# A graph layer and a mixture of experts: the first two node tiles go through all eight experts unsorted

## The chip, the cores and the metric

The kernel runs on one core of one Trainium2 chip. A core has TensorE (PE: matmuls and transposes), VectorE (DVE), ScalarE (ACT), GpSimd (POOL) and SyncE (SP, which here only issues transfers). Each has its own queue of instructions and takes them in order; they wait for one another through semaphores. Transfers run on 16 DMA engines. The metric is the device time of one execution in microseconds (us).

## The reference

There are 6250 nodes of 256 features, 100000 edges of which only the first 6250 matter to the output, and eight experts. Cut to what matters:

```python
def gnn(x, edge_index, weight, attn_l, attn_r):       # 4 heads of 64
    xt = (x @ weight).reshape(-1, 4, 64)
    alpha_l = einsum('ehd,hd->eh', xt[row], attn_l)
    alpha_r = einsum('ehd,hd->eh', xt[col], attn_r)
    alpha = softmax(leaky_relu(alpha_l + alpha_r, 0.01), axis=1)
    tmp = einsum('nh,nhd->nd', alpha[:n], xt[col[:n]])
    return broadcast_to(tmp[:, None, :], (n, 4, 64)).reshape(n, 256)

def moe(tokens, router_w, w1, b1, w2, b2):
    probs = softmax(tokens @ router_w.T)
    rw, re = top_k(probs, 2);  rw = rw / rw.sum(-1)
    combine = zeros((n, 8)).at[arange(n)[:, None], re].set(rw)
    out = tokens
    for e in range(8):
        h = gelu(tokens @ w1[e] + b1[e])               # 256 -> 256
        out = out + combine[:, e:e+1] * (h @ w2[e] + b2[e])
    return out

x = x + gnn(layernorm(x), stack([src, dst]), ...)
return x + moe(layernorm(x), ...)
```

Each node needs two of the eight experts. All of it is in float32.

## The kernel before

The nodes lie in 49 tiles of 128. The work is a straight program, written out in the order in which every engine is to take it; no scheduler reorders it. It has four stages.

**Setup and source terms** (to about 48 us). The rows of x, the edges and the graph weight are loaded, and per node the source side of the attention and the router's share of the node's own row are computed.

**Features** (48 to 139 us). The 49 tiles come in five groups, `GROUPS`, of 10, 10, 9, 10 and 10. GpSimd gathers the rows of the destination nodes; TensorE turns them (`turn`), multiplies them by the graph weight (`features`) and looks up the source terms (`look_up`); ScalarE copies each product and squares each row; VectorE does the attention and the routing. The work after the matmuls of a group is spread over the tiles of the next one by `tasks(g)`: `attend_1`, `exponents` (ScalarE), `attend_2`, `attend_3` and the five steps of `route` for group g-1, `rank` (TensorE) and `ranked` (VectorE) for group g-2. `put(i, what)` sets the tile after which a piece stands. `route` finds the two best experts of each node, writes the group's finished rows into `table` in DRAM, and marks in `mine_all` which of the 28 pairs of experts the node belongs to. `rank` counts, with matmuls of ones, how many nodes of the same pair come earlier. `feature_root` is a power on GpSimd at the end of each group, which `attend_1` needs.

**The sort** (139 to 191 us). The last group has no next one to hide in: `attend_1(z)`, `exponents(z)`, `rank(z - 1)`, `ranked(z - 1)`, `attend_2(z)`, `attend_3`, `route(z)`, `rank(z)`, `ranked(z)` come one after the other. Then VectorE turns the ranks into places (`place`), and with one-hot tables in bfloat16 (`of_lane`, `of_slice`, `by`, in three passes) and 49 matmuls (`pi`) the places are inverted: `held_by` names the node in each place. The nodes now lie in 49 slices of 128, ordered by pair. The pairs follow the path `PATH`, in which neighbours share an expert, so that a slice holds few experts. A slice and an expert that it needs make a *unit*; there are at most 2 x 49 + 28 - 1 = 125, `NU`. `pf` (16 matmuls) makes the list of units; VectorE turns it into integers, `for_act`, `for_pe` and `for_dve`, that the engines read as registers. A Gelu on one element (`warm`) brings ScalarE's table in early, and `keep_on(26)` issues 26 matmuls whose results nobody reads.

**The sorted units** (191 to 433 us). `fetch` gathers sorted rows from `table` (an indirect DMA on GpSimd), `norm` normalizes them on VectorE, GpSimd and ScalarE, and `turn_slice` turns them. For unit u, `fill` loads the expert's first matrix (256 KB, on SP's queue, 4 units ahead, six buffers), `first` does its 4 matmuls and two Gelus, and `second`, two units later, the 2 matmuls by `we2` (all experts' second matrices, held in `big`) and two scaled additions into `acc` on VectorE. `finish` scatters a slice's rows to the output with an indirect DMA. The queue of SP between the stages holds, in this order: the table write of group 3 (L593), the one of group 4, the register load of `for_act` (L1051), and the loads of the first units (L1079).

Memory is reused across stages: `early.close()` frees the tiles of the first three stages, and the tiles of the units (`late`) lie where those were.

Of the kernel before, what the change touches and what calls it, by code (L numbers as in the profile page):

```python
# [9 lines left out]
FP = mybir.dt.float32  # L10
BF = mybir.dt.bfloat16
# [11 lines left out]
def kernel(  # L23
# [35 lines left out]

    nc = tc.nc  # L60
    N, D = x.shape
# [21 lines left out]
    NS = -(-N // TS)  # L83
# [17 lines left out]
    assert sum(n for _, n in GROUPS) == NT == NS and HD == D and F == D and NE == 8  # L101
    assert 96 <= LAST < P

    const = ctx.enter_context(tc.tile_pool(name="const", bufs=1))
# [14 lines left out]


# [10 lines left out]
    held_by = const.tile([TS, NS], I32, name="held_by")  # L131

# [20 lines left out]
    mine_all = held.tile([P, NT, NPAIR], BF, name="mine_all")  # L153
    rank_all = held.tile([P, NT], FP, name="rank_all")
    outside = held.tile([P, 1], FP, name="outside")

    NTE = NT + NT % 2
    high_1 = held.tile([P, NTE * P], BF, name="high_1")
# [396 lines left out]
    table = dram.tile([NT * P, R], FP, name="table")  # L555
# [3 lines left out]
    def route(g):  # L559
# [33 lines left out]
        nc.sync.dma_start(table_v[:, at, :], row)  # L593
# [3 lines left out]
        mine = mine_all[:, at, :]  # L597
        nc.vector.tensor_tensor(mine, long(pairs, n), wide(pair, NPAIR), ALU.is_equal)
# [6 lines left out]
    def rank(g):  # L605


        n, mine = GROUPS[g][1], mine_all[:, group(g), :]
# [14 lines left out]
    def ranked(g):  # L623
        n, pk = GROUPS[g][1], ranks.pop(g)
# [4 lines left out]
        nc.vector.tensor_tensor(mr, pk[:, :n, :], mine_all[:, group(g), :], ALU.mult)  # L629
        nc.vector.tensor_reduce(rank_all[:, group(g)], mr, AX.X, ALU.add)  # L630
        if g == NG - 1:
            nc.vector.tensor_tensor(
                rank_all[:, NT - 1 :], rank_all[:, NT - 1 :], outside, ALU.add
            )
# [73 lines left out]
    count_b = mid.tile([P, NTE], BF, name="count_b", bufs=1)  # L708
    def counting():
# [5 lines left out]
            count_b, pattern=[[1, NTE]], base=0, channel_multiplier=0,  # L715
            allow_small_or_imprecise_dtypes=True,
        )

# [7 lines left out]
    def tasks(g):  # L726
# [22 lines left out]
        if g == 3:  # L749
            put(0, load_experts)  # L750
        if g == 4:
            put(0, load_biases)
        return at
# [30 lines left out]
    n = GROUPS[z][1]  # L784
    attend_1(z)
    exponents(z)
    rank(z - 1)
    ranked(z - 1)
# [14 lines left out]

    warm = small.tile([P, 1], FP, name="warm", bufs=1)
    nc.scalar.activation(warm, exs[z][:, 0, :1], AF.Gelu)
# [9 lines left out]
    ms = work.tile([P, NT, NPAIR], FP, name="ms", tag="pxs")  # L815
    for g in range(NG):
        nc.vector.tensor_tensor(
            ms[:, group(g), :], mine_all[:, group(g), :],
# [7 lines left out]
    for k, (op, by) in enumerate(  # L826
# [5 lines left out]
        if NTE > NT:  # L832
            nc.vector.memset(part[:, NT:], -1.0)
# [366 lines left out]
```

## Time and profile before

| | |
|---|---|
| median of 9 runs | 441.67 us (439.25 to 442.88) |
| the profiled execution | 444.69 us, its span 442.9 us |
| mean granted TensorE clock | 0.931 |
| TensorE matmul, busy | 377.1 us (85%) |
| VectorE, busy | 311.0 us (70%) |
| ScalarE, busy | 224.9 us (51%) |
| GpSimd, busy | 200.6 us (45%) |
| last look-up matmul ends / first sorted unit starts | 138.92 / 190.97 us |

Line numbers L... are those of the kernel before. In a group of the profile, `out<-in` names what an instruction writes and reads; PE is a matmul, PEld a weight load. One float32 matmul is counted as two, so a unit's `first` is 8 and its `second` 4. The granted clock is 1.00 where TensorE runs at full speed and 0.50 at half. The chain of waits is the work that ended last, followed back from the end: an engine that is not in it had time to spare there.

### The profile page before, as it was taken

To read this page: it belongs to the slowest core of one execution; us is meant where nothing else is said; L and a number is where in the kernel's file an instruction comes from. 1 tells how busy PE (TensorE), PEld (TensorE's weight loads), DVE (VectorE), ACT (ScalarE), POOL (GpSimd) and SP (SyncE) were. 2 spreads that over 40 slices of the span, in tenths; PEclk is the share of its full clock that TensorE was granted. 3 is DMA by queue.
4 is the path that set the end of the run, shared out by engine and by line. 5 is a ranking of instruction groups with operands and counts; after the bars stand their busy time and mean duration, and the time that the engine had idled before them with its cause. 6 is when DMAs were issued, how large, how long until landed. Compare 5 with 4: busy or idle time off the path is not lost.

```text
span 442.9 us, 9881 instructions
## 1 busy us (share of the span) xinstructions
PE 377.1 (85%) x2576; PEld 323.6 (73%) x2576; DVE 311.0 (70%) x1083; ACT 224.9 (51%) x658; POOL 200.6 (45%) x240
## 2 busy tenths in 40 slices
PE   6977869998995018878999999999998999999991
PEld 4754648776784016467999998888887899999990
DVE  5979512889879987537888778778677877655551
ACT  3454547865773100056666666656556567433330
POOL 0075867888222000543434366657556643332222
PEclk9996999999999555689999999999999999999997
DMA  7978443473971440386666676667766656666620
GB/s 228 354 202 109 78 84 63 88 214 109 295 222 53 144 156 0 97 243 165 195 182 180 196 228 184 219 206 218 218 191 206 202 186 191 180 183 193 187 71 22
DMA packets 59108, 74.63 MB, mean 169 GB/s; under 512 B 7170, under 2 KB 54102, under 8 KB 58800
## 3 DMA queue, kind: packets, MB, share of 16 engines
q1 hardware_dynamic: 51504, 52.45, 38.9%
q0 software_dynamic: 7248, 21.29, 18.9%
q8 instruction: 23, 0.38, 0.3%
q10 hardware_dynamic: 304, 0.27, 0.2%
q14 instruction: 29, 0.24, 0.2%
HBM read 59.13 MB, written 14.87 MB: 167 GB/s over the span
## 4 chain that ended last, share of the span: by engine, by line
PE 69%; DVE 16%; issue 5%; ACT 3%; DMA 2%; POOL 1%; another core or an unknown queue 1%; SPq 1%; POOLq 0%; ACTq 0%
PE ph L1091 26%; PE py L1107 23%; PE px L468 6%; PE pt L246 4%; DVE pxs L544 3%; PE pt L1037 2%; DVE pxs L549 2%; PE pa L422 2%; PE pl L497 1%; DVE x L550 1%; PE pi L856 1%; ACT tT L250 1%; DMA w<-in_L_ffn_w_dram 1%; DVE ag L505 1%
## 5 line engine op out<-in xcount | busy, mean ns | idle before, releaser
L1091 PEld LDWEIGHTS ph<-tokT,w 128*128 128x128 f32 x1000 | 131.1, 194 | 18.9 <-issue 5.4
L1091 PE MATMUL ph<-tokT,w 128*128 (+1 forms) x1000 | 134.6, 278 | 7.4 <-ACT tokT L1038 2.1
L1107 PE MATMUL py<-big,hid 128*128 x500 | 128.9, 381 | 0.0
L1098 ACT ACTIVATE hid<-ph,b_cols 128x128 f32<-128x128 f32 x250 | 78.5, 366 | 84.3 <-PE ph L1091 67.0
L1107 PEld LDWEIGHTS py<-big,hid 128*128 128x128 f32 x500 | 85.4, 191 | 7.4 <-DVE acc L1114 0.6
L914 POOL DMA_INDIRECT xr<-table,held_by x49 | 49.8, 1017 | 74.3 <-DVE held_by L901 39.2
L1114 DVE SCALAR_TENSOR_TENSOR acc<-py,shares,acc 128x256 f32 (+1 forms) x125 | 60.5, 484 | 32.3 <-PE py L1107 13.7
L1118 POOL DMA_INDIRECT out_dram<-acc,held_by x49 | 51.0, 1040 | 54.8 <-DVE acc L1114 39.7
L1114 DVE SCALAR_TENSOR_TENSOR acc<-big,shares,acc (+1 forms) x125 | 60.2, 481 | 11.0 <-issue 5.3
L468 PE MATMUL px<-w_sb,tT 128*128 128x293 f32 x196 | 57.2, 423 | 4.1 <-issue 3.8
L1004 ACT ACTIVATE tok<-xr,nm 128x256 f32<-128x256 f32 x49 | 29.4, 602 | 58.1 <-DVE nm L1000 41.1
L468 PEld LDWEIGHTS px<-w_sb,tT 128*128 128x128 f32 x196 | 34.7, 193 | 12.2 <-issue 4.7
L235 POOL DMA_INDIRECT big<-in_x_dram,dst_sb x31 | 33.0, 1064 | 7.9 <-issue 7.2
L250 ACT COPY tT<-pt 128x512 f32<-128x512 f32 (+2 forms) x56 | 27.3, 528 | 14.6 <-PE pt L246 13.2
L476 ACT COPY pxs<-px 128x293 f32<-128x293 f32 x49 | 19.7, 403 | 27.9 <-PE px L468 17.1
L978 DVE TENSOR_TENSOR xr<-xr 128x512 f32<-128x512 f32 (+1 forms) x25 | 17.2, 689 | 17.6 <-issue 17.5
L1014 ACT ACTIVATE acc<-xr,nm 128x256 f32<-128x256 f32 x49 | 29.1, 597 | 0.0
L505 DVE TENSOR_REDUCE ag<-pl 128x8 f32<-128x392 f32 (+1 forms) x25 | 13.8, 552 | 18.2 <-PE pl L501 12.7
L993 POOL TENSOR_SCALAR mv<-mv 128x2 f32<-128x2 f32 (+1 forms) x25 | 5.6, 225 | 39.0 <-DVE mv L990 35.2
L235 POOL DMA_INDIRECT xd_own<-in_x_dram,dst_sb x18 | 19.3, 1070 | 4.9 <-issue 4.1
L246 PE MATMUL pt<-ident,x 128*128 128x128 f32 x98 | 17.3, 328 | 4.5 <-ACT tT L250 2.3
L497 PE MATMUL pl<-al_sb,high 128*128 128x196 bf16 x147 | 19.2, 251 | 1.9 <-DVE ag L505 1.9
(210 smaller groups left out, 479.8 us busy)
## 6 DMA issues: line engine op xcount, KB each, us to landing
w<-in_L_ffn_w_dram SPq DMA_DIRECT2D x125, 256.0 KB
table<-x SPq DMA_DIRECT2D x4, 1685.0 KB
x<-in_x_dram SPq DMA_DIRECT2D x10, 512.0 KB
big<-in_L_ffn_w_dram SPq DMA_DIRECT2D x2, 1024.0 KB
high<-highs SPq DMA_DIRECT2D x1, 1568.0 KB
table<-x SPq DMA_DIRECT2D x1, 1516.5 KB
big<-in_L_ffn_b_dram SPq DMA_DIRECT2D x1, 1024.0 KB
xr<-table,held_by POOLq DMA_INDIRECT x49
```

The source lines that it names most:

```text
L235: nc.gpsimd.indirect_dma_start(out=xd(t), out_offset=None, in_=x[:, :], in_offset=bass.IndirectOffsetOnAxis(ap=dst_sb[:, t : t + 1], axis=0),)
L246: nc.tensor.transpose(pt[:, i * P : (i + 1) * P], of(t0 + i)[:, c * 128 : (c + 1) * 128], ident)
L250: nc.scalar.copy(tT, pt)
L468: nc.tensor.matmul(px, blocks[c][:, k * P : (k + 1) * P], w_sb[:, c, :], start=(c == 0), stop=(c == DC - 1),)
L914: nc.gpsimd.indirect_dma_start(out=xr[:, i, :], out_offset=None, in_=table[:, :], in_offset=bass.IndirectOffsetOnAxis(ap=held_by[:, s0 + i ...
L1004: nc.scalar.activation(tok[:, i, :], xr[:, i, :D], AF.Identity, bias=bias[:, i : i + 1], scale=scale[:, i : i + 1],)
L1014: nc.scalar.activation(acc[:, s * D : (s + 1) * D], xr[:, i, :D], AF.Identity, bias=bias[:, i : i + 1], scale=more[:, i : i + 1],)
L1091: nc.tensor.matmul(ph[:, j, :], w[:, c * F + j * 128 : c * F + (j + 1) * 128], tokT[:, bass.ds(rows_at + c * TS, TS)], start=(c == 0), sto ...
L1098: nc.scalar.activation(hid[:, j, :], ph[:, j, :], AF.Gelu, bias=b1_cols[:, :, j][:, bass.ds(at_act[u][0], 1)])
L1107: nc.tensor.matmul(py, hid[:, j, :], we2[:, j, bass.ds(at_pe[u][1], D)], start=(j == 0), stop=(j == FC - 1),)
L1114: nc.vector.scalar_tensor_tensor(to, y, share, to, op0=ALU.mult, op1=ALU.add)
L1118: nc.gpsimd.indirect_dma_start(out=ends_at[s][:, :], out_offset=bass.IndirectOffsetOnAxis(ap=held_by[:n, s : s + 1], axis=0), in_=acc[:n, ...
```

## The change

Tiles 0 and 1 of the nodes no longer take part in the sort. Their rows stay in SBUF (`xs[0]`), and after the features they go through all eight experts, with a share of 0 for the six that a node does not use: 16 unsorted units, `UNSORTED`. For the rest there are 47 tiles and slices (`NTS`, `NS`), so `NU` is 121, and every table of the sort is narrower by two columns. `group(g)` becomes `sorted_of(g)` where sorted tiles are meant.

- `load_unsorted` loads the eight first matrices (2 MB) and b2 on SP's queue into memory of groups 1 and 2 that is free by then: six matrices in group 3, two and b2 in group 4.
- `complete`, `sums`, `squares`, `scaled` do the layer norm of the two tiles on GpSimd and ScalarE, among the tiles of group 4.
- `turn_unsorted` turns them; `unsorted_shares` makes the shares; `unsorted_units(n)` takes n steps of the 17: step k is `unsorted_first(k)`, then `unsorted_second(k - 1)`. A result is copied out of PSUM with its share as scale by ScalarE (`y`, three buffers) and added to `d_acc` by GpSimd.
- The steps are put between the pieces of the sort, 2 + 2 + 3 + 4 + 1 + 5, with the bias terms after the fourth. The last five take the place of 20 of the 26 matmuls of `keep_on`.
- `warm` moves ahead, to just behind `exponents(z)`.
- At the end of the last step the two tiles are stored, on SP's queue.
- `finish` scatters by `held_out`, the places moved by 256 rows.

```diff
-    NS = -(-N // TS)
+    ND = 2
+    NTS = NT - ND
+    NS = -(-(N - ND * P) // TS)
     NU = 2 * NS + NPAIR - 1
...
+    UNSORTED = [(d, e) for d in range(ND) for e in range(NE)]
...
+    def load_unsorted(k):
+        e0, e1 = ((0, 6), (6, NE))[k]
+        of = held.tile([128, (12, 11)[k] * D], FP, name=f"unsorted{k}", tag=f"x{k + 1}")
+        for e in range(e0, e1):
+            w1_parts[e] = of[:, (e - e0) * DC * F : (e - e0 + 1) * DC * F]
+            nc.sync.dma_start(w1_parts[e].rearrange("p (c f) -> p c f", f=F),
+                w1[e : e + 1, :, :].rearrange("o (c p) f -> p (o c) f", p=128))
...
+            nc.sync.dma_start(d_of["b2"], b2)
+    def complete():
+        for d in range(ND):
+            v = d_row[:, d, :D].rearrange("p (h k) -> p h k", k=OC)
+            nc.gpsimd.tensor_tensor(
+                v, v, d_row[:, d : d + 1, U : U + OC].to_broadcast([P, H, OC]), ALU.add)
+    def sums():
+        for d in range(ND):
+            nc.scalar.activation(
+                d_y[0], d_row[:, d, :D], AF.Identity, accum_out=d_sum[:, d : d + 1])
+        nc.gpsimd.tensor_scalar(d_mean, d_sum, -ROOT_D / D, None, ALU.mult)
+    def squares():
...
+        root(d_scale, d_var)
...
+    def scaled():
+        for to, by in ((d_tok, d_scale), (d_acc, d_more)):
+            for d in range(ND):
+                nc.scalar.activation(to[d], d_row[:, d, :D], AF.Identity,
+                    bias=d_bias[:, d : d + 1], scale=by[:, d : d + 1])
+    def turn_unsorted():
...
+    def unsorted_shares():
+        nc.scalar.activation(d_second, d_log, AF.Tanh, scale=0.5)
...
+    def unsorted_first(k):
+        d, e = UNSORTED[k]
+        w, tokT = w1_parts[e], d_of["tokT"]
+        ph = ps.tile([128, FC, P], FP, name="ph4", tag="m")
...
+        hid = d_of["hid"][k % 3]
+        for j in range(FC):
+            nc.scalar.activation(hid[:, j * P : (j + 1) * P], ph[:, j, :], AF.Gelu,
+                bias=b1_cols[:, e, j : j + 1])
+    def add_to(d, k, py, scale):
+        y = d_y[k % 3]
+        nc.scalar.activation(y, py, AF.Identity, scale=scale)
+        nc.gpsimd.tensor_tensor(d_acc[d], d_acc[d], y, ALU.add)
+    def unsorted_second(k):
...
+        add_to(d, k, py, d_share[:, d, e : e + 1])
+    def unsorted_biases():
+        for d in range(ND):
+            pt = ps.tile([NE, P], FP, name="pt5", tag="t")
+            nc.tensor.transpose(pt, d_share[:, d, :], ident)
+            to = d_of["shareT"][:, d * P : (d + 1) * P]
+            nc.scalar.copy(to, pt)
+            py = ps.tile([P, D], FP, name="py5", tag="t")
+            nc.tensor.matmul(py, to, d_of["b2"], start=True, stop=True)
+            add_to(d, d, py, 1.0)
+    def unsorted_units(n):
+        for k in range(gone[0], min(gone[0] + n, len(UNSORTED) + 1)):
+            if k < len(UNSORTED):
+                unsorted_first(k)
+            if k > 0:
+                unsorted_second(k - 1)
+        gone[0] += n
+        if gone[0] == len(UNSORTED) + 1:
+            for d in range(ND):
+                nc.sync.dma_start(out_parts[NS][d * P : (d + 1) * P, :], d_acc[d])
...
         if g == 3:
             put(0, load_experts)
+            put(5, lambda: load_unsorted(0))
         if g == 4:
             put(0, load_biases)
+            put(1, lambda: load_unsorted(1))
+            for i, what in ((1, complete), (3, sums), (5, squares), (8, scaled)):
+                put(i, what)
...
+    turn_unsorted()
     attend_1(z)
     exponents(z)
+    warm = small.tile([P, 1], FP, name="warm", bufs=1)
+    nc.scalar.activation(warm, exs[z][:, 0, :1], AF.Gelu)
+    unsorted_shares()
+    unsorted_units(2)
     rank(z - 1)
+    unsorted_units(2)
+    unsorted_biases()
+    unsorted_units(3)
     ranked(z - 1)
...
-    warm = small.tile([P, 1], FP, name="warm", bufs=1)
-    nc.scalar.activation(warm, exs[z][:, 0, :1], AF.Gelu)
+    unsorted_units(4)
...
-    for t0, t1 in ((0, 10), (10, 24), (24, NTE)):
+    for t0, t1 in ((0, 10), (10, 24), (24, NTO)):
+        if t0 == 10:
+            unsorted_units(1)
...
-    keep_on(26)
+    unsorted_units(5)
+    keep_on(6)
...
+    nc.vector.tensor_scalar(held_out, held_by, ND * P, None, ALU.add)
     early.close()
```

## The prediction

> **What bounds the kernel now.** I read the page's slices first (the span in 40 equal parts; a digit is the busy share in tenths, or the granted clock), then the chain of waits, then the timeline and the chain around the valley that the slices show.
>
> ```profile
> PE   6977869998995018878999999999998999999991
> ...
> DVE  5979512889879987537888778778677877655551
> ...
> PEclk9996999999999555689999999999999999999997
> ...
> PE 69%; DVE 16%; issue 5%; ACT 3%; DMA 2%; POOL 1%; another core or an unknown queue 1%; SPq 1%; POOLq 0%; ACTq 0%
> ```
>
> TensorE is full in the feature stage (to about 139 us) and in the sorted units (from 201 us). Between them, slices 13 to 17, it is nearly idle and its clock falls to half: there VectorE sorts the nodes, and the chain runs through VectorE. A microsecond there costs as much as one in a unit. The price of a unit is read in the steady part of the chain (start, length, what):
>
> ```profile
> 419.13 0.89 PE ph L1091 x8
> 420.02 0.87 PE py L1107 x4
> 420.89 0.89 PE ph L1091 x8
> ```
>
> A unit is 0.89 + 0.87 = 1.76 us of TensorE with nothing in between. While slices are still turned, two units take 3.73 us (chain starts 225.94 to 229.67), so a turned slice adds 0.22.
>
> The valley's ends decide this case. The timeline where the features end:
>
> ```profile
> 143.29 0.40 PE L611 MATMUL rank<-mine_all,ones_b 128*128 128x280 bf16 x1
> ...
> 144.76 0.24 ACT L526 ACTIVATE ex<-lr 128x40 f32<-128x40 f32 x1 [6.22 <-DVE lr L520]
> 144.98 0.18 DVE L625 TENSOR_TENSOR counts<-counts,rank 128x28 f32<-128x28 f32 x1 [0.25 <-PE rank L617]
> 145.02 1.28 ACT L805 ACT_TABLE_LOAD   x1
> ```
>
> The fourth group's ranks (from 143.26) are done when VectorE wants them: it waits 0.25 us at 144.98. The other end, in the chain:
>
> ```profile
> 172.86 4.81 PE pi L856 x25
> ...
> 179.53 1.85 PE pf L929 x16
> ...
> 182.16 0.38 DVE for_act L939
> ...
> 182.75 0.55 SPq L1051
> ...
> 186.52 4.31 DMA w<-in_L_ffn_w_dram
> 190.83 0.14 issue
> 190.97 3.56 PE ph L1091 x16
> ```
>
> Unit 0 waits for its weights, not for its nodes (turned by 189.63). From the expert list on VectorE (for_act, ready at 182.54) to the first matmul it is 8.43 us: SP reads registers and issues the first load at 186.52, which lands 4.31 later. From the end of pf (181.38) it is 9.59 us.
>
> **The change part by part.**
>
> 1. *Fewer units.* 47 sorted slices give 2x47+27 = 121 units instead of 125: 4 x 1.757 + 2 x 0.22 = **-7.5 us**, all on the bound. This is the whole direct gain; the 16 new units (28 us of TensorE) must fit in the valley's idle time.
>
> 2. *ScalarE and GpSimd in group 4.* Sums and squares are 4 x (0.51 + 0.19, the pair of L478), scaled is 4 x 0.60 (L1004): 5.2 us on ScalarE between 130 and 138.5, where its gaps are 0.6 to 0.7 us each. Walking its queue with them in place, the last tile's square ends at 142.0 instead of 138.5. GpSimd's root (0.25 + 1.98, pace of 138.62 to 140.94) then ends at 144.5, and attend_1, at 143.60 before, waits: +0.9. TensorE is not held: its last look-up ended at 138.92, 4.2 us before VectorE took it. The two whole-row adds on GpSimd (complete) precede all this with over 10 us of GpSimd idleness in front. If gaps absorb more, 0; if less, 2. **+0.9 (0 to 2).** The 2 MB of added loads use SP and DMA between 113 and 143, where DMA stands at 0.52 and 0.10 in the stretches 128:140 and 140:144; SP's next urgent issue is the table write at 142.7. Nothing; without that cover at most the transfer, 2 MB at 350 GB/s, 6 us.
>
> 3. *rank(3) is queued behind the first two steps on TensorE.* The program order is: turn, first(0), first(1), second(0), rank(3). second(0) needs gelu(0) on ScalarE, and that stands behind exponents(4), which needs attend_1. So from attend_1's end: exp 0.24, table load 1.28, warm and tanh 0.35, two gelus 0.63 (a pair of L1098), handovers 0.1: 2.6 us; second(0) 0.87, or 1.74 at half clock; the rank block 0.95, or 1.70 as at 143.26 to 144.96. VectorE, whose next instruction is ranked(3), gets it 4.4 to 6.0 us after attend_1 instead of 0.25; some 0.2 of its own handover falls away. attend_2 to the last mine_all stand behind it. TensorE will have been idle about 3.7 us by then; the clock fell 4.1 us after the last matmul at 138.9. Between the ends I take **+5.0 (4.2 to 5.8).**
>
> 4. *rank(4) behind five units and the biases.* 5 x 1.757 = 8.8; the biases go PE, ScalarE, PE twice over (a copy 0.26 and a y of 0.6 each, plus the y before): 2.6; together 11.4. VectorE needs 144.98 to 156.50 = 11.5 to reach it. So it just fits at full clock; starting at half it is 1.4 late. The rank itself falls from 1.70 to 0.95. **0.0 (-0.8 to +1.4).**
>
> 5. *The sort.* Group 0 has 8 tiles, the lanes 48 columns instead of 50 (third pass 24 of 26 of 3.82 us): -0.5. The last pi has 23 matmuls instead of 25, at 0.19: -0.4. Four units (7.0) lie in the 8.4 us between rank(4) and the first pi, one between two passes. The clock is the open point: pi and pf at full speed would take 2.2 and 0.9 less. In before, pi was busy for 8.1 of the 11 us to 177.7 and the clock stayed at 0.5 until 183.9, when dense 512-column matmuls had run. I take the row: once the valley lets the clock drop ahead of the last pass, pi does not lift it. **-0.9 (-4.0 to +1.0)**, the upper end for GpSimd's adds disturbing VectorE, which no row here shows.
>
> The Trainium skill (TensorE: Matmul & The Clock Gate, "What's actually happening") says that about 3.4 us of sustained activity releases the clock. By it, pi's own 4.8 us would have been enough, and the sum would be 3.1 lower; the trace's 0.50 in that stretch says otherwise.
>
> 6. *SP waits for the last sum.* Both stores of the unsorted rows are on SP's queue, ahead of the reading of for_act and of all weight loads. The second waits for GpSimd's last add. After pf come five steps: 4 x 0.89 + 5 x 0.87 = 7.9 us at full clock, some 2.5 more if they begin at half: 9.1. Then y 0.65, the add, store issue 0.45 (SP's static issues take 0.37). The add has no row; 256 elements at iota's rate (5.25 us for 3328, one stream) are 0.4, and three such streams 1.2: I take 0.7. So SP begins at 10.9 after pf, where for_act was there 1.16 after it. Its own 8.43 to the first matmul follow: 19.3 against 9.59, **+9.7 (8.2 to 11.5).** VectorE's clearing of shares, and with it slice 0's normalization, now waits for the last unsorted matmul as well, but is ready some 4 us before the weights, as the weights are last today. keep_on(6) hides behind the same wait.
>
> The Trainium skill (GPSIMD Engine Reference, "Engine selection") advises against elementwise adds on GpSimd and gives 4497 ns for 2048 elements; an estimate from it is 0.56 us for this add, which would put the sum 0.1 lower. No row here shows one.
>
> 7. *The ramp* (190.97 to 201.28) keeps its chain: gelus, copy, tanh, accumulators, GpSimd's fetch, normalization. The weights no longer share DMA with five fetches: **-0.5 (-1.5 to 0).**
>
> Sum: -7.5 + 0.9 + 5.0 + 0.0 - 0.9 + 9.7 - 0.5 = **+6.7 us.** The profiled execution took 444.69 (span 442.9, 1.8 around it), so it would be 451.4; the runs' median is 441.67, 3.0 below the profiled one, so 441.67 + 6.7 = **448.4**.
>
> **The rivals.**
>
> *Full clock throughout (faster).* If the unsorted matmuls hold the clock at 1.0 from 143 us through the first sorted units, item 3 falls to 4.2, item 4 to -0.75, item 5 to -4.0, item 6 to 8.5, and units 0 and 1 need 1.78 instead of 3.56: together 8.6 less, **-1.9 us, 439.8**. For it: dense matmuls raised the clock at 183.9. Against it: the clock fell again at 190.8, although TensorE had been at work until 188.4 and at two transposes after that, and the wait of item 6 is longer. It turns faster once it saves more than 6.7, and by 0.3% from 8.0.
>
> *One wait is covered.* If SP's 8.43 us shrinks because its register work or the landing is quick without competition (landing 2 instead of 4.31, say, and half of the 4 us before it), item 6 is 4.3 less: +2.4, 444.1. For it: 0.86 MB of fetches shared those microseconds. Against it: SP had waited 26.4 us in before too, and still took 4 us.
>
> *The units do not fit.* If GpSimd's adds take about 2.5 us beside VectorE's two-input work, three y buffers make 2.5 the pace of a unit: seven sums before rank(4) take 17.5 instead of 11.4, four units 10.0 where 8.4 are free, and the five last some 2 more: +6.1 + 1.6 + 2, so 458. For it: this kernel has no such add to read. Against it: fetches on GpSimd took 0.95 to 1.1 us beside VectorE.
>
> **How the numbers follow.** Forecast 0.64, full clock 0.12, one wait covered 0.14, not fitting 0.10. The first and last are slower. Of the covered case four fifths are slower by more than 0.3% (1.3 us, about what this kernel's runs can tell from no change) and the rest within; of the full clock half is faster, half within. Slower 0.85, within 0.09, faster 0.06. The forecast's own bounds, not all at one end at once, reach from 444 to 453; with the covered wait, and half of the other two cases left out, the range is 442.0 to 454.0.
>
> **What would show it.** In the profile after: VectorE's ranked(3) waiting 4 us or more for rank, with the gelu table load ahead of it in the chain; the second store on SP issued 10 to 12 us after pf, the first sorted unit 18 to 21 after it; 121 units at 1.76; the clock near 1.0 in the valley's middle, and 0.5 or 1.0 in the last pi, which settles item 5. The forecast is wrong if VectorE runs through ranked(3), or if the first weights land less than 14 us after pf.

## The result, and the profile after

The changed kernel takes 453.95 us (median of 15 runs, 451.76 to 456.07), the kernel before in the same comparison 441.27 us (46 runs): 1.029 times as long, with an interval of 1.0273 to 1.0307. That is 12.7 us more. The forecast was 448.4 with a range of 442.0 to 454.0: the direction was right, the size was half. The profiled execution of the changed kernel took 453.9 us with a span of 452.1, against 444.69 and 442.9 before, so the two profiles differ by 9.2 us. The profile of before was 3.0 above the median of the nine runs that the forecast had, 3.4 above that of the 46; that of the changed kernel stands at its median.

The slices and the chain's shares by engine, from the page of the changed kernel:

```profile
PE   5968869998995997895899999999999999999991
...
DVE  5979312987986789214689777777887687555552
...
PEclk9897989999997898586999999999999999999997
...
PE 48%; issue 2%; POOL 1%; DMA 1%; ACT 1%; POOLq 0%; DVE 0%; ACTq 0%; SPq 0%
```

This chain can be followed back to 202.84 us only, so its shares say nothing of the valley. The empty valley of before (TensorE at 0 and 1 tenths in slices 14 and 15) is filled: 9 and 9. But the sorted units begin at 209.01 us where they began at 190.97, so 18.0 us are lost ahead of them, and from there to the end 8.8 are won (251.93 to 243.1). Four stretches between the pairs of the fourth group (mine_all, 142.76 before, 141.34 after) and the first sorted unit hold the loss. In the table, "pairs to ranked(3)" ends where VectorE takes the fourth group's ranks, "to ranked(4)" where it takes those of the last group. All figures are us, and the runs of the next section are in it already. Beside some of them (after_again, stores_late, own_memory, reordered, adds_aside, stride_128) the kernel before took 441 us and beside the others 428.5, so times are compared as ratios to the kernel before, measured beside each run, and profiles by these stretches.

| kernel | pairs to ranked(3) | to ranked(4) | to the end of pf | to unit 0 | sum |
|---|---|---|---|---|---|
| before | 2.22 | 13.29 | 23.10 | 9.60 | 48.21 |
| changed | 7.66 | 14.99 | 27.90 | 17.12 | 67.67 |
| changed, again (after_again) | 7.78 | 14.32 | 27.60 | 16.97 | 66.67 |
| rank_first | 2.22 | 20.40 | 27.93 | 17.71 | 68.26 |
| stride | 7.78 | 14.99 | 25.46 | 17.34 | 65.57 |
| small_adds | 7.72 | 14.30 | 26.52 | 16.20 | 64.74 |
| no_between | 7.78 | 14.93 | 24.69 | 18.07 | 65.47 |
| stores_late | 7.59 | 14.98 | 27.85 | 16.80 | 67.22 |
| own_memory | 7.62 | 14.92 | 27.93 | 14.66 | 65.13 |
| reordered | 2.22 | 14.93 | 24.66 | 13.25 | 55.06 |
| adds_aside | 2.04 | 12.69 | 22.62 | 11.02 | 48.37 |
| early_root | 2.23 | 12.88 | 22.62 | 11.93 | 49.66 |
| stride_128 | 7.78 | 14.31 | 24.43 | 17.00 | 63.52 |
| stride_by | 7.78 | 15.01 | 24.33 | 16.62 | 63.74 |

*The first two stretches.* VectorE's timeline in the changed kernel (start, length, line, operation, out and in, and in brackets the idle time ahead and who ended it):

```profile
149.00 0.18 DVE L642 TENSOR_TENSOR counts<-counts,rank 128x28 f32<-128x28 f32 x1 [5.70 <-PE rank L633]
...
154.05 2.06 DVE L561 TENSOR_TENSOR pxs<-pxs 128x1440 f32<-128x1440 f32 x1
156.15 1.32 DVE L562 TENSOR_TENSOR x<-pxs 128x720 f32<-128x720 f32 x1
157.50 0.65 DVE L588 TENSOR_TENSOR logits<-own_r,x 128x80 f32<-128x80 f32 x1
...
163.99 0.18 DVE L642 TENSOR_TENSOR counts<-counts,rank 128x28 f32<-128x28 f32 x1 [0.91 <-PE rank L633]
```

The wait of item 3 is there: 5.70 us instead of 0.25. Behind it, three operations take 2.06, 1.32 and 0.65, and some of the short ones behind them grow alike. The same three in the kernel before, and GpSimd's adds, which run beside them in the changed kernel:

```profile
150.03 1.66 DVE L549 TENSOR_TENSOR pxs<-pxs 128x1440 f32<-128x1440 f32 x1
151.72 0.91 DVE L550 TENSOR_TENSOR x<-pxs 128x720 f32<-128x720 f32 x1
152.67 0.24 DVE L576 TENSOR_TENSOR logits<-own_r,x 128x80 f32<-128x80 f32 x1
```

```profile
151.47 7.25 POOL L848 TENSOR_TENSOR big<-big 128x256 f32<-128x256 f32 x4 [2.54 <-ACT big L847]
```

*The sort.* TensorE's timeline from the first pass to pf:

```profile
173.74 2.53 PE L1037 MATMUL pi<-by,of_lane 128*128 128x94 bf16 x10 [2.66 <-DVE by L1033]
176.08 1.90 PE L834 MATMUL ph<-unsorted,unsorted 128*128 128x128 f32 x8
177.78 1.84 PE L855 MATMUL py<-big,unsorted 128*128 128x256 f32 x4
179.45 8.83 PE L1037 MATMUL pi<-by,of_lane 128*128 128x94 bf16 x37
...
190.11 1.78 PE L1110 MATMUL pf<-is_unit,fields 47*1 47x121 bf16 x16 [1.71 <-DVE is_unit L1077]
```

Before, the passes ran as 10, 14 and 25 matmuls, and the last 25 took 4.81 us. Now the unsorted step between the first two passes takes 3.4 us at half clock, the 14 of the second pass come behind it, and 37 stand in a row behind the last product (179.46). Each also takes longer: 8.83 us for 37 is 0.239 each (here and below, the length of a row over its number of matmuls; from one start to the next the trace has 0.23 to 0.24), where it was 0.193.

*From pf to the first unit.* SP's queue, VectorE's timeline, and the chain of waits (start, length, what):

```profile
169.04 35.00 SPq L883 DMA_DIRECT2D out_dram<-big  x2
206.17 9.13 SPq L1262 DMA_DIRECT2D w<-in_L_ffn_w_dram  x9
```

```profile
193.85 0.17 DVE L1134 TENSOR_SCALAR held_out<-held_by 128x47 int32<-128x47 int32 x1
202.43 0.41 DVE L1140 MEMSET shares<- 128x423 f32 x1 [8.41 <-PE py L855]
204.30 0.43 DVE L1161 TENSOR_TENSOR xr<-xr 128x256 f32<-128x256 f32 x1 [1.46 <-issue]
```

```profile
204.74 0.26 SPq L1234
...
206.17 2.70 DMA w<-in_L_ffn_w_dram
208.87 0.14 issue
209.01 3.77 PE ph L1274 x16
```

SP sits in the two stores for 35.00 us. But VectorE waits as well, 8.41 us, before it may clear shares, because that tile lies on memory that the unsorted tiles' operands hold until the last unsorted matmul. Slice 0's turned nodes were ready at 208.66, 0.35 us before unit 0.

### The profile page after: what moved, and what is told of

It reads as the page before. It is cut to its first block, busy times and chain, and to the rows that moved or that the text cites. A ratio compares the mean times of both kernels' runs of the same rounds, so it can differ in the third digit from the quotient of the medians.

```text
span 452.1 us, 10184 instructions
## 1 busy us (share of the span) xinstructions
PE 402.7 (89%) x2702; PEld 347.0 (77%) x2702; DVE 308.4 (68%) x1064; ACT 243.2 (54%) x710; POOL 220.5 (49%) x266
## 3 DMA queue, kind: packets, MB, share of 16 engines
HBM read 59.84 MB, written 14.52 MB: 164 GB/s over the span
## 4 chain that ended last, share of the span: by engine, by line
PE 48%; issue 2%; POOL 1%; DMA 1%; ACT 1%; POOLq 0%; DVE 0%; ACTq 0%; SPq 0%
PE ph L1274 24%; PE py L1290 22%; PE pt L1220 2%; DMA w<-in_L_ffn_w_dram 1%; POOL xr L1095 0%; POOLq L1378 0%; POOL nm L1177 0%; ACTq L1234 0%; ACT acc L1197 0%; POOL out_dram L1301 0%; ACT hid L1281 0%; DVE stats L1171 0%; DVE acc L1297 0%; POOL mv L1176 0%; DVE xr L1161 0%
## 5 line engine op out<-in xcount | busy, mean ns | idle before, releaser
L1274 PEld LDWEIGHTS ph<-tokT,w 128*128 128x128 f32 x968 | 127.3, 194 | 16.4 <-issue 5.1
L1274 PE MATMUL ph<-tokT,w 128*128 (+1 forms) x968 | 130.5, 279 | 5.5 <-ACT tokT L1221 2.3
L1290 PE MATMUL py<-big,hid 128*128 x484 | 124.8, 381 | 0.0
L1281 ACT ACTIVATE hid<-ph,b_cols 128x128 f32<-128x128 f32 x242 | 75.8, 365 | 80.4 <-PE ph L1274 69.2
L1290 PEld LDWEIGHTS py<-big,hid 128*128 128x128 f32 x484 | 82.7, 191 | 7.0 <-DVE acc L1297 0.4
L1301 POOL DMA_INDIRECT out_dram<-acc,held_out x47 | 49.1, 1044 | 53.4 <-DVE acc L1297 37.7
L1095 POOL DMA_INDIRECT xr<-table,held_by x47 | 47.8, 1017 | 43.2 <-issue 11.3
L1297 DVE SCALAR_TENSOR_TENSOR acc<-big,shares,acc (+1 forms) x121 | 58.3, 482 | 8.7 <-issue 3.2
L1187 ACT ACTIVATE tok<-xr,nm 128x256 f32<-128x256 f32 x47 | 28.1, 600 | 20.5 <-POOL nm L1177 14.5
L848 POOL TENSOR_TENSOR big<-big 128x256 f32<-128x256 f32 x18 | 17.8, 991 | 23.8 <-ACT big L847 23.5
L841 ACT ACTIVATE unsorted<-ph,b_cols 128x128 f32<-128x128 f32 x32 | 9.9, 364 | 29.8 <-PE ph L834 16.0
```

The lines of the kernel that those rows point to most:

```text
L1095: nc.gpsimd.indirect_dma_start(out=xr[:, i, :], out_offset=None, in_=table[:, :], in_offset=bass.IndirectOffsetOnAxis(ap=held_by[:, s0 + i ...
L1187: nc.scalar.activation(tok[:, i, :], xr[:, i, :D], AF.Identity, bias=bias[:, i : i + 1], scale=scale[:, i : i + 1],)
L1274: nc.tensor.matmul(ph[:, j, :], w[:, c * F + j * 128 : c * F + (j + 1) * 128], tokT[:, bass.ds(rows_at + c * TS, TS)], start=(c == 0), sto ...
L1281: nc.scalar.activation(hid[:, j, :], ph[:, j, :], AF.Gelu, bias=b1_cols[:, :, j][:, bass.ds(at_act[u][0], 1)])
L1290: nc.tensor.matmul(py, hid[:, j, :], we2[:, j, bass.ds(at_pe[u][1], D)], start=(j == 0), stop=(j == FC - 1),)
L1297: nc.vector.scalar_tensor_tensor(to, y, share, to, op0=ALU.mult, op1=ALU.add)
```

## The experiments

Ratios to the kernel before stand with their 95% intervals. Edits are shown against the changed kernel, that of early_root against adds_aside, and "..." marks lines left out.

**1. rank_first.** The fourth group's ranks go ahead of the unsorted steps.

```diff
-    unsorted_units(2)
     rank(z - 1)
-    unsorted_units(2)
+    unsorted_units(4)
```

> The changed kernel with one move: the ranks of the fourth group are issued on TensorE ahead of the first steps of the unsorted tiles instead of behind two of them. In the changed kernel VectorE waits 5.70 us for them at 149.00. Theory (the wait is on the path, as item 3 of the forecast has it): VectorE's ranked(3) waits about 0.3 us, the sort and all behind it start some 5.4 us earlier, and of the 454.0 us about 4 to 5.4 go: 448.6 to 450. Rival (the time of the stretch is set by GpSimd's adds and VectorE's two-input operations standing in each other's way, and by the adds' own pace): the rank of the last group becomes late instead, because the seven steps ahead of it take as long as before, and no more than 2 us go: 452 or more. The stretch from ranked(3) to ranked(4) tells: 15.0 us in the changed kernel; about 15 by the theory, 18 or more by the rival.

Measured: 1.0337 (1.0291 to 1.0383), so nothing was won. VectorE's timeline has the wait gone from one place and back at the next:

```profile
135.26 0.18 DVE L642 TENSOR_TENSOR counts<-counts,rank 128x28 f32<-128x28 f32 x1 [0.25 <-PE rank L633]
...
137.10 3.16 DVE L556 TENSOR_TENSOR pxs<-pxs,alpha 128x2880 f32<-128x2880 f32 x1
140.29 1.66 DVE L561 TENSOR_TENSOR pxs<-pxs 128x1440 f32<-128x1440 f32 x1
...
155.66 0.18 DVE L642 TENSOR_TENSOR counts<-counts,rank 128x28 f32<-128x28 f32 x1 [6.66 <-PE rank L633]
```

GpSimd's and TensorE's timelines tell why:

```profile
137.26 4.87 POOL L822 TENSOR_SCALAR d_share<-x,d_nm 128x8 f32<-128x8 f32 x2
142.21 0.76 POOL L826 TENSOR_TENSOR d_share<-d_share,x 128x16 f32<-128x16 f32 x1
```

```profile
143.79 1.13 PE L855 MATMUL py<-big,unsorted 128*128 128x256 f32 x4 [1.72 <-ACT unsorted L841]
```

Two tiny operations on GpSimd, 0.62 us together in the changed kernel, take 4.87. The first takes 3.19 beside VectorE's operation of 3.16 us (L556), which now starts just ahead of it, the second 1.69 beside the one of 1.66 (L561), and each ends 0.2 us after that operation. ScalarE needs the shares to take the first y from TensorE's result (it waits until 143.01), the next gelus stand behind that, and TensorE waits for the gelus. The seven steps and the biases ahead of rank(4) thus end 19.4 us after ranked(3), and VectorE gets the ranks 20.40 us after it, within the rival's "18 or more". Item 3's wait is real, but it is not additive: in this order the 5.4 us taken from one wait came back on the other, by way of the late shares.

**2. stride.** The three tiles that pi's matmuls read (of_lane, of_slice and by, all three edited alike) are 50 columns wide again.

```diff
+    NTW = 50
-    of_lane = held.tile([P, TS, NTO], BF, name="of_lane", tag="high_1")
+    of_lane = held.tile([P, TS, NTW], BF, name="of_lane", tag="high_1")
...
```

> The changed kernel with the three tiles that the sort's 47 matmuls read (lanes, slices, their product) allocated 50 columns wide again, of which 48 are computed, so the step between two elements that one matmul reads is 100 bytes as before and not 96. In the changed kernel one of these matmuls starts every 0.239 us, at clock 1.00 as at 0.50; before, every 0.193 us at 0.50. Theory (the step of the reads sets their pace): 0.193 again, the last 37 take 7.1 instead of 8.8 us, and the time falls by 1.5 to 2.2 us, to about 452. Rival (the pace is set by something else that the change brought, the clock or the other units' traffic): 0.24 stays and the time stays within 0.5 us of 454.

Measured: 1.0271 (1.0224 to 1.0318), which the times alone don't tell from the changed kernel. In the profile, the stretch from ranked(4) to pf is 25.46 instead of 27.90 (27.60 in the repeat), by the faster matmuls:

```profile
165.22 1.98 PE L1038 MATMUL pi<-by,of_lane 128*128 128x94 bf16 x10 [2.65 <-DVE by L1034]
...
170.45 6.88 PE L1038 MATMUL pi<-by,of_lane 128*128 128x94 bf16 x37
```

6.88 us for 37 is 0.186 each. So the step of the reads sets the pace, and a table that had become two columns narrower made each of its matmuls a quarter slower.

**3. small_adds.** GpSimd adds 8 of 256 columns; the kernel leaves the rest of these sums out.

```diff
-        nc.gpsimd.tensor_tensor(d_acc[d], d_acc[d], y, ALU.add)
+        nc.gpsimd.tensor_tensor(d_acc[d][:, :8], d_acc[d][:, :8], y[:, :8], ALU.add)
```

> The changed kernel in which GpSimd adds only 8 of 256 columns of each expert's output to the sums of the unsorted tiles (it leaves the rest of these sums out). Theory (GpSimd's adds and VectorE's operations with two inputs in on-chip memory stand in each other's way): VectorE's operations between ranked(3) and the sort go back to their lengths of before (the 2.06 us one to 1.66, the 1.32 to 0.91, those of 0.59 to 0.79 to about 0.2), ranked(3) to the last pairs takes 11.1 us instead of 13.4, and the time falls by 2.5 to 4 us; another 0.7 us goes behind pf, as the second store waits for the last add. Rival (VectorE's lengths come from waits inside them or from ScalarE and TensorE reading the same memory): the lengths stay, and only the 0.7 us at the end go.

Measured: 1.0289 (1.0246 to 1.0331), no gain that the times show. On VectorE the theory holds to the hundredth:

```profile
146.34 1.66 DVE L561 TENSOR_TENSOR pxs<-pxs 128x1440 f32<-128x1440 f32 x1
148.03 0.91 DVE L562 TENSOR_TENSOR x<-pxs 128x720 f32<-128x720 f32 x1
...
155.60 0.18 DVE L642 TENSOR_TENSOR counts<-counts,rank 128x28 f32<-128x28 f32 x1 [2.49 <-PE rank L633]
```

The lengths are those of before, and the pairs of the last group come 11.09 us after ranked(3), as before (11.06; 13.36 in the changed kernel). But rank(4) isn't reached yet on TensorE, VectorE waits 2.49 us for it, and only 0.7 us or less is left of the gain at ranked(4). The expected 2.5 to 4 us overlooked that. From ranked(4) to the last product VectorE takes 14.03 us, where the changed kernel takes 15.47 and the kernel before 14.52: here the adds cost 1.4. In the profile the first sorted unit comes 64.74 us after the pairs, 1.9 to 2.9 less than in the changed kernel's two.

**4. no_between.** No step between two passes of the sort, six behind pf.

```diff
-        if t0 == 10:
-            unsorted_units(1)
...
-    unsorted_units(5)
+    unsorted_units(6)
```

> The changed kernel without the unsorted step between the first and the second pass of the sort; six steps instead of five follow pf. Theory (that step ran at half clock, 176.1 to 179.6, and held the 14 matmuls of the second pass on TensorE until the third pass was ready, so that 37 stood in a row): the last product of the sort to the last matmul of pi takes 5.5 us instead of 8.8, while one more step stands ahead of the second store (1.76 us): 1 to 2 us less, 452 to 453. Rival (the matmuls of pi are late for their own pace of 0.239 us, whatever is between them): the stretch falls by less than 1 us, and the further step makes the time 0.5 to 1.8 us longer than the changed kernel's.

Measured: 1.0301 (1.0257 to 1.0344). All 47 matmuls run in one row:

```profile
166.53 11.32 PE L1035 MATMUL pi<-by,of_lane 128*128 128x94 bf16 x47 [2.66 <-DVE by L1031]
```

The last product to the end of pi takes 5.6 us, as expected; ranked(4) to pf is 3.2 shorter (24.69), and pf to the first unit 0.95 longer (18.07). The stretch to unit 0 is 65.47 instead of 67.67 or 66.67; the times don't resolve that. With all 47 behind one another the clock can be read too: from 170 to 177.8 us TensorE did nothing but pi, and the granted clock was 0.50 throughout.

**5. after_again and stores_late.** The changed kernel once more, and the same with the stores issued during the ninth sorted unit.

```diff
-        if gone[0] == len(UNSORTED) + 1:
-            for d in range(ND):
-                nc.sync.dma_start(out_parts[NS][d * P : (d + 1) * P, :], d_acc[d])
...
+        if u == 8:
+            store_unsorted()
```

> The changed kernel itself, for a profile and times on the chip that the runs beside it are made on. Both theories: 1.029 times the kernel before (1.027 to 1.031), 28 us from ranked(4) to the end of pf and 17 from there to the first sorted unit.

> The changed kernel with the two stores of the unsorted rows issued by SP eight sorted units later, behind the weight loads of these units instead of ahead of all. Theory of the forecast's item 6 (SP's queue is what the first sorted unit waits for, its nodes are ready some 4 us before its weights): from the end of pf to the first unit 13 us instead of 17, and about 4 us less in all (450). Rival (the first unit's nodes wait for the memory that the unsorted tiles' weights and activations hold until the last unsorted matmul, so they are as late as the weights): 16 to 17 us, and at most 1 us less.

Measured: 1.0331 (1.0294 to 1.0367) and 1.0324 (1.0288 to 1.0359). The stretches of the repeat differ from those of the first profile by 0.1 to 0.7 us each, which is what differences in the table should be held against. With late stores nothing moves, 16.80 us instead of 16.97:

```profile
202.89 0.41 DVE L1141 MEMSET shares<- 128x423 f32 x1 [8.40 <-PE py L855]
```

SP issues its first weight load at 202.84, at the moment at which VectorE gets the memory too. Item 6's queue was not what held unit 0, or not it alone.

**6. own_memory.** Besides late stores, the last steps' weights, activations and shares get tiles of their own; the steps go expert by expert. d_w1 holds the weights of experts 6 and 7, and the turned tokens take the place of d_tok.

```diff
+    d_w1 = const.tile([128, 2 * DC * F], FP, name="d_w1")
+    d_hid = const.tile([128, 3 * D], FP, name="d_hid")
+    d_share = const.tile([P, ND, NE], FP, name="d_share")
-    UNSORTED = [(d, e) for d in range(ND) for e in range(NE)]
+    UNSORTED = [(d, e) for e in range(NE) for d in range(ND)]
...
```

> As the run with the late stores, and besides the last unsorted steps read and write only tiles that the sorted units' tiles do not lie on (weights of the last two experts, activations, shares; the steps go expert by expert, both tiles each, for that). Theory (memory): clearing of shares and the add and the statistics of slice 0 on VectorE run right behind for_act, 6 us or more before the last unsorted step; what is left behind the last step is the root on GpSimd behind the last add, tok, the turn and the copy, some 2.9 us after the last add at 11.8, so the first unit starts 14.5 to 15 us after pf instead of 17.1, and about 2.4 us go against the changed kernel. Rival (SP's queue alone): no more than the run with late stores.

Measured: 1.0267 (1.0229 to 1.0304), against 1.0331 and 1.0324 beside it; the medians are 452.36, 454.79 and 454.48 us, 2.1 to 2.4 less. pf to unit 0 is 14.66, within the expected 14.5 to 15. VectorE and GpSimd in this run:

```profile
195.05 0.41 DVE L1140 MEMSET shares<- 128x423 f32 x1 [0.23 <-issue]
...
205.49 0.16 DVE L1179 TENSOR_TENSOR nm<-nm,xr 128x1 f32<-128x1 f32 x1 [7.48 <-POOL nm L1177]
```

```profile
202.87 1.59 POOL L847 TENSOR_TENSOR big<-big 128x256 f32<-128x256 f32 x2 [1.03 <-ACT big L846]
204.55 0.25 POOL L1176 TENSOR_SCALAR mv<-mv 128x1 f32<-128x1 f32 x1
```

VectorE clears shares 2.35 us after pf instead of 10.5. What waits now is the root of slice 0, queued on GpSimd behind the last add. So three things held the first unit at nearly the same time: SP's queue, last by 0.35 us in the changed kernel, the memory, and GpSimd's queue. What SP's queue alone would cost, with the memory free, no run shows.

**7. reordered.** All of it at once: shares with exp ahead of gelu's table, rank(3) first and rank(4) behind five steps, 50 columns, own memory, late stores, no step between two passes; behind pf three steps, the reading of the lists, one step, the turn of slice 0, one step, and two among the first sorted units. VectorE adds the last two results. `A_STEPS` and `B_STEPS` are 5.

```diff
     turn_unsorted()
+    unsorted_shares()
     attend_1(z)
     exponents(z)
...
-    unsorted_shares()
-    unsorted_units(2)
     rank(z - 1)
-    unsorted_units(2)
-    unsorted_biases()
-    unsorted_units(3)
+    unsorted_units(4)
+    turn_shares()
+    unsorted_units(A_STEPS - 4)
     ranked(z - 1)
...
     rank(z)
+    unsorted_units(1)
+    unsorted_biases()
     ranked(z)
...
-    unsorted_units(4)
+    unsorted_units(B_STEPS - 1)
...
-    unsorted_units(5)
-    keep_on(6)
...
+        if u in (2, 3):
+            unsorted_units(1)
```

> All causes at once: ranks of group 4 first on TensorE, the unsorted shares taken with exp ahead of the group's softmax instead of tanh behind it, ranks of the last group behind five steps instead of seven and the biases, no step between two passes of the sort, tiles of 50 columns, own memory, late stores, and ten steps ahead of pf, four between pf and the turn of slice 0, one behind it and two among the first sorted units. If the causes named (late ranks 5.4 and with them the shares, the sort's matmuls 4.8, memory and SP 7.5) are the right ones, the first sorted unit starts 48 to 54 us after the fourth group's pairs are found (48.2 before, 67.7 in the changed kernel) and the kernel takes 0.98 to 1.0 of the time before. If they are not, it stays above 1.01.

Measured: 1.0013 (0.9987 to 1.0039), no longer slower than before. 11.6 to 12.6 us of the 18.5 to 19.5 that the changed kernel loses ahead of the first unit are back (55.06), a little less than expected. VectorE's timeline shows one part of the rest:

```profile
144.66 0.18 DVE L646 TENSOR_TENSOR counts<-counts,rank 128x28 f32<-128x28 f32 x1 [0.26 <-PE rank L637]
...
149.70 2.07 DVE L565 TENSOR_TENSOR pxs<-pxs 128x1440 f32<-128x1440 f32 x1
151.80 1.31 DVE L566 TENSOR_TENSOR x<-pxs 128x720 f32<-128x720 f32 x1
...
159.59 0.18 DVE L646 TENSOR_TENSOR counts<-counts,rank 128x28 f32<-128x28 f32 x1 [1.51 <-PE rank L637]
```

Now that rank(4) is not late, the lengthened operations lie on the path.

**8. adds_aside.** The adds go to where VectorE waits; the last six are VectorE's own. Nine more y buffers lie in the place of x2. Six steps instead of five stand ahead of the last group's ranks, and behind pf four are left ahead of the first sorted unit instead of five. With that much moved at once, the rows and not the time say what the adds did.

```diff
-        y = d_y[k % 3]
+        y = d_of["y"][k]
         nc.scalar.activation(y, py, AF.Identity, scale=scale)
-        nc.gpsimd.tensor_tensor(d_acc[d], d_acc[d], y, ALU.add)
+        waiting.append((k, d, y))
...
+    add_waiting(2, mine_all[:, NTS - 1, :1])
     rank(z)
...
+    add_waiting(7, by[:, 1, 0, NTO - 1 : NTO])
     edge = small.tile([NS, 2], FP, name="edge", bufs=1)
```

> The reordered kernel with GpSimd's adds moved to where VectorE waits or has short work: outputs of the unsorted experts are kept in nine further buffers, two adds run behind the last group's pairs, seven behind the last product of the sort, three among the sorted units, and the last six are taken by VectorE from TensorE's result directly; ranks of the last group stand behind six steps instead of five, and slice 0's root stands ahead of the adds on GpSimd. Theory (the adds cost VectorE some 0.4 us each where they meet its two-input operations): ranked(3) to the last pairs 11.1 us instead of 13.2, ranked(4) to the last product 14.5 to 15 instead of 16.6, pf 4 us earlier, and 0.985 to 0.992 of the time before. Rival (the lengthening comes from ScalarE's and TensorE's traffic, which stays): both stretches stay within 0.5 us, and only the smoother start of the units is left, 0.995 to 1.0.

Measured: 0.9893 (0.9855 to 0.9931), 1.1% under the kernel before, with an interval that leaves 1 out. VectorE, GpSimd and TensorE:

```profile
149.38 1.66 DVE L565 TENSOR_TENSOR pxs<-pxs 128x1440 f32<-128x1440 f32 x1
151.08 0.91 DVE L566 TENSOR_TENSOR x<-pxs 128x720 f32<-128x720 f32 x1
```

```profile
156.40 1.41 POOL L861 TENSOR_TENSOR big<-big,unsorted 128x256 f32<-128x256 f32 x2
...
171.28 5.12 POOL L861 TENSOR_TENSOR big<-big,unsorted 128x256 f32<-128x256 f32 x7
```

```profile
167.17 8.68 PE L1061 MATMUL pi<-by,of_lane 128*128 128x94 bf16 x47
```

ranked(3) to the pairs is 11.06, ranked(4) to the last product 13.98 (14.52 before), and pf ends 4.5 us earlier after the fourth group's pairs than in the reordered kernel (37.35 and 41.81). The first sorted unit is where it was before (48.37 and 48.21), 15 of the 17 unsorted steps are done by then, and the four units saved are kept. The seven adds behind the last product still lengthen three short operations of VectorE (0.67, 0.66 and 0.85 where the reordered kernel has 0.24, 0.18 and 0.38), but pi is at work until 175.85 and VectorE waits for TensorE behind them.

**9. early_root.** Only the order behind pf.

```diff
-    unsorted_units(1)
+    unsorted_first(gone[0])
     name_units(0)
...
     go_on(0, 2)
-    unsorted_units(2)
+    unsorted_second(gone[0] - 1)
+    gone[0] += 1
+    unsorted_units(1)
     go_on(0, 1)
+    unsorted_units(1)
```

> The run with the adds aside, and behind pf only the order changed: the first of the remaining steps is split so that the engines read the expert lists, and VectorE takes slice 0's add and statistics, ahead of the first add that waits for TensorE; slice 0's tok is issued one step earlier on ScalarE. In the run before, TensorE waited 1.57 us at 187.07 for slice 0's tok and 1.29 us at 192.83 for slice 1's turned nodes. Theory (both waits come from VectorE's queue: xr's add stood behind a wait for TensorE and 1.5 us of register loads): both waits fall below 0.5 us each and 1 to 2.5 us go, 0.984 to 0.988 of the time before. Rival (the nodes of slice 1 wait for GpSimd's fetches and ScalarE's gelus anyway): one of the two waits stays or grows, and the time stays within 0.5 us of 0.989.

Measured: 0.9903 (0.9871 to 0.9936), the same as the run before, which is the rival's outcome. The first wait (1.40 us for slice 0's tok in the run before) is gone and another stands ahead of it: ScalarE takes the gelus of this step late; the second wait (1.29 there) stays, and the first unit starts 11.93 us after pf instead of 11.02:

```profile
173.37 2.04 PE L868 MATMUL py<-big,d_hid 128*128 128x256 f32 x4 [0.79 <-ACT d_hid L843]
...
186.72 1.16 PE L1297 MATMUL ph<-tokT,w 128*128 x8 [1.34 <-ACT tokT L1244]
```

**10. stride_128 and stride_by.** The changed kernel with all three tiles 64 columns wide (the edit of stride with 64 in the place of 50), and with only the moving operand so, which is this:

```diff
-    by = work.tile([P, 2, NS, NTO], BF, name="by", tag="pxs")
+    by = work.tile([P, 2, NS, 64], BF, name="by", tag="pxs")
```

> The changed kernel with the sort's three tiles allocated 64 columns wide, so that one of its matmuls reads elements 128 bytes apart (96 in the changed kernel, 0.239 us from start to start; 100 in the run with 50 columns). If a step that is a multiple of 32 bytes is slow, 0.239 us or more; if only small differences in width matter or the wider the slower, something between; if the step does not matter at all, the 0.19 of the run with 50 columns was chance and this run shows 0.19 or 0.24 without order.

> The changed kernel with only the moving operand of the sort's matmuls (the products) 64 columns wide, elements 128 bytes apart; the stationary operand (the lanes) keeps 48 columns, 96 bytes. If the moving operand's step sets the pace, one matmul starts every 0.165 us as with all tiles 64 wide; if the stationary one's does, every 0.239 us as in the changed kernel.

Measured: one time each, 448.68 us (the kernel before 440.58 beside it) and 438.14 (428.6), from which no ratio is taken. TensorE's timeline of the first and of the second:

```profile
177.92 6.10 PE L1038 MATMUL pi<-by,of_lane 128*128 128x94 bf16 x37
```

```profile
169.69 6.48 PE L1037 MATMUL pi<-by,of_lane 128*128 128x94 bf16 x37
```

0.165 and 0.175 us each, from one profile of either. So it is not that multiples of 32 bytes are slow: 128 is faster than 100, and 96 is the slowest of the three. Most of it is the moving operand's step, which alone takes 0.064 of the 0.074 us away; the stationary operand's step alone was not varied. To the end of pf these two kernels take 24.43 and 24.33 us instead of 27.60 to 27.90.

## Why the prediction was wrong in size

Point by point, in the profiles (the signs add up to the 9.2 us between the two spans):

- *Items 1 and 7* (-8.0): behind the first sorted unit the changed kernel is 8.8 us shorter, 7.5 in the repeat. Right.
- *Item 2* (+0.9): no cost. The fourth group's pairs come at 141.34 instead of 142.76 (-1.4), and at 141.3 in the repeat. ScalarE and GpSimd took the extra work in their gaps: the last tile's square ended at 139.02, not at 142.0.
- *Item 3* (+5.0): +5.4, by the mechanism named. What the sum did not say is that this wait and item 4's cover one another: rank_first took it away and won nothing.
- *Item 4* (0.0): +1.7, +1.0 in the repeat. The step's two bounds held for TensorE; VectorE's own part grew by 2.3 us through GpSimd's adds and fell by 0.6 through the faster rank.
- *Item 5* (-0.9, with +1.0 as the upper end): **+4.8, and this is the step that failed.** It priced the last pass as "23 matmuls instead of 25, at 0.19", a price taken from matmuls that read every 100 bytes, for matmuls that read every 96; and it let a step lie "between two passes" at no cost, which took 3.4 us at a granted clock of 0.50 and held the second pass. The first made 0.239 of 0.193 (stride gives back 2.4 us, or 2.1 against the repeat), the second put 14 more matmuls behind the last product (no_between gives back 3.2, or 2.9). Of the 4.8, 3.85 lie behind the last product (8.58 to the end of pf before, 12.43 now), and only 0.95 on VectorE ahead of it (14.52 and 15.47), where the upper end of 1.0 was meant to stand for the adds: that part was sized right (small_adds has 14.03 there, so the narrower tables gave the forecast 0.5 and the adds took 1.4), the matmuls had no upper end at all.
- The clock, on which item 5 spent its thought, did not set the pace of pi. Its matmuls started every 0.23 to 0.24 us at a granted clock of 1.00 (174 to 176, and 179.5 to 182.8) and at 0.50 (183 to 188.2) alike, so the 2.2 us that full speed was to take off pi are shown by no run. The clock cost something elsewhere: the step between the passes took 3.4 us at 0.50, where one at full clock takes 1.76, an estimated 1.6 us. The reading that pi does not lift the clock held: TensorE was full of pi from 183 to 188.2 and in no_between from 170 to 177.8, both at 0.50. The Trainium skill's rule weighed there (TensorE: Matmul & The Clock Gate, "What's actually happening") would have had pi lift the clock after some 3.4 us; in these rows it did not. In the kernel before, pi's three rows fill 9.7 of the 11 us to 177.7, not 8.1, which makes the same point more strongly.
- *Item 6* (+9.7): +7.5. The wait for the last step is there, but both prices and the reason were off. SP was through with the second store 12.2 us after pf instead of 10.9. From its register reading to the first issue it then took 1.4 us instead of 3.77, and the load landed in 2.70 instead of 4.31, which is the rival of the covered wait. And slice 0's nodes were not "ready some 4 us before the weights" but 0.35 us: the memory held them too (stores_late against own_memory).

In the profiles, then, the forecast of 451.4 met 453.9. That this is no further off is luck in part: items 3 to 5 came 7.8 us above the sum, 5.7 of them in item 5, and items 1, 2, 6 and 7 together 5.3 below it. The larger miss in the medians, 12.7 against 6.7, has a second source: the kernel before was 3.4 us above the median of its 46 runs when it was profiled, and the sum took that execution's rows. Its fourth group's pairs came at 142.76, where the seven profiles of the changed kernel and its variants beside which it took 441 us have 141.1 to 142.4; where the rest of the 3.4 us lies, no run shows.

Of the rivals, that of units that do not fit named the right engine: GpSimd's adds and VectorE's two-input work do exclude each other. Its place was wrong: the pace of a step did not become 2.5 us, VectorE's own chain grew. The rival of the full clock was added up wrongly: its five terms make 7.6 us and not 8.6, which would have been -0.9 and 440.8.

## What to carry to other kernels

When work is put into an idle valley, price it against every queue that the valley's critical engine shares, memory included: here one change made several waits that cover one another, and taking away any one of them won nothing or 1 to 4 us in the stretch to the first sorted unit, while all together, with the adds moved, turned 1.029 into 0.989. A row's duration holds for its operands' layout; when a dimension of a tile changes, even to a smaller one, its price has to be asked again. And put small adds on GpSimd where VectorE waits, not where it works.

## What the runs showed of the hardware that was not expected

- A bf16 matmul with 94 columns that gathers single elements took 0.239 us (a row's length over its number) when they lay 96 bytes apart, 0.186 at 100 and 0.165 at 128, and 0.175 with only the moving operand's elements 128 apart. The Trainium skill (SBUF — State Buffer, "Door 1") speaks of lines of 16 bytes and a penalty for each access to a new one; by that the three steps would cost the same, and they do not. Why 96 is slow stays open.
- GpSimd's add of 128x256 takes 0.72 us alone, and four of them took 7.25 us beside VectorE's two-input operations, while VectorE lost about 0.4 us per meeting. In rank_first two tiny share products took 3.19 and 1.69 us instead of 0.62 together, beside two such operations of 3.16 and 1.66 that did not grow. The Trainium skill (GPSIMD Engine Reference, "Specifications") says that the two share their interfaces to on-chip memory and collide on VectorE instructions with two inputs there; the rows agree and give the price.
